# A decoder kernel: the feed-forward's first pair of token tiles is prepared in the last steps of the cross attention, and side jobs are pinned in DVE's queue

## The chip, the cores and the metric

The kernel runs on one core of a Trainium2 chip. The metric is the device time of one execution in microseconds (us), less is better. The engines are named as in the profile: PE (TensorE, matrix products and transposes), DVE (VectorE), ACT (ScalarE), POOL (GpSimd) and SP (SyncE, which here only issues DMAs). Each runs its own queue in order; semaphores make one wait for another.

## The reference

The reference is a decoder of two layers over 16 sequences of 128 tokens with 512 features. Each of its six parts is followed by a residual add and a layer norm: a state-space scan, a cross attention with 16 heads, a feed-forward with ternary weights and 8-bit activations, a causal attention with ternary weights ("BitLinear"), a gated cross attention and a mixture of experts. The change touches the seam between the second and the third part. The third is:

```python
def _L0_ffn_ref(x, W_g, W_u, W_d):
    def rms_norm(x, eps=1e-08):
        mean = jnp.mean(x, axis=-1, keepdims=True)
        var = jnp.var(x, axis=-1, keepdims=True)
        return (x - mean) / jnp.sqrt(var + eps)
    def activation_quant(x):
        s = 127.0 / jnp.max(jnp.abs(x), axis=-1, keepdims=True)
        return jnp.clip(jnp.round(s * x), -128, 127) / s
    def ternary_matmul(x, w):
        return jnp.matmul(x, jnp.sign(w).T)
    xq = activation_quant(rms_norm(x))
    g = jax.nn.silu(ternary_matmul(xq, W_g))
    u = ternary_matmul(xq, W_u)
    p = g * u
    return ternary_matmul(p, W_d)
...
x = _layernorm(x + _L0_xattn_ref(x, ctx_2048, ...), axis=-1)
x = _layernorm(x + _L0_ffn_ref(x, L0_ffn_W_g, L0_ffn_W_u, L0_ffn_W_d), axis=-1)
```

W_g and W_u are 2048 x 512, W_d is 512 x 2048.

## The kernel before

The tokens stay on the chip as 16 tiles `k.x[b]` of 128 tokens by 512 features. The stages run one after another over all 16 tiles; within the program the order on each engine is made by a scheduler from priorities (program order) and estimated costs, so an instruction whose inputs are ready can be put ahead of others that stand earlier in the program. An instruction handed to `keep_in_program_order` is not moved in this way.

**Cross attention** (`stage_xattn`, profile lines L450 to L614). One step handles a pair of heads of one tile; there are 128 such units, 8 per tile. A step computes scores (L555), maxima (L559), exponentials (L568, ACT), the normalization by the sums (L574, and L575 on POOL) and the transposes of the probabilities (L583), whose results ACT (L586) and DVE (L588) copy to `pTs`. The generator `outputs` makes the attention output `ao` (L595), its copy `aT` (L600) and the product with Wo, `po` (L606); after the last head group `po` is added to the token tile (L609) and, when both tiles of a pair are done, the pair is normalized (`layernorm`, L68 to L72). Side generators in the list `running` are advanced once per step: the projections of the next tile (`project`, with `rope` at L450 to L460) and the like. The last units belong to tiles 14 and 15. Its PSUM takes two banks each for projections (`pp`), scores (`psc`), transposes (`ppt`), and two for `ao` and `po`.

**Feed-forward** (`stage_ffn`). It works over pairs of tiles. `prepare` normalizes a pair (`xn`), finds each token's largest magnitude (L680), scales and rounds (`q_t`, L690, DVE, by adding a large constant; `q_q`, L691, ACT, by taking it away), transposes the result (L701, PE) and copies it (`q_T`, L703, ACT). The first pair is prepared before the loop; each later one in the loop, one piece at a time. In the loop, for each tile and each of four blocks of 512 hidden features, PE makes the gate and up products `pg` and `pu` (L755), ACT the Silu `sg` (L758), DVE the product `sg` (L759), PE its transposes (L375), ACT and DVE split them into `hi` (L764) and `lo` (L765), and PE adds their products with the down weights into `po` (L769), which is added to the token tile (L777). `load_ffn_weights` loads the weights through five rotating slots and ACT takes their signs (L659 for gate and up, L669 for down).

**Side jobs.** `ahead` holds work for the next stage: `load_bit_weights` (sums of magnitudes L807, then the ternary weights L820 to L822) and `load_gated_masks` (a maximum over the mask L834, the mask values L837 and L839). In the program the generator is advanced in the second half of a tile's blocks, from the second pair of tiles on; in the order that the scheduler makes, L807 and L834 to L839 stand at the start of the stage.

Of the kernel before, what the change touches and what calls it, by code (L numbers as in the profile page):

```python
# [10 lines left out]
F32 = mybir.dt.float32  # L11
BF16 = mybir.dt.bfloat16
# [3 lines left out]
AF = mybir.ActivationFunctionType  # L16
ALU = mybir.AluOpType
AX = mybir.AxisListType
PSUM = bass.MemoryType.PSUM

P = 128
NB = 16
D = 512
KC = D // P
NT = NB * P
MAGIC = 12582912.0
# [377 lines left out]
def stage_xattn(k):  # L404
# [9 lines left out]
    with ExitStack() as ctx:  # L414
# [175 lines left out]
        def outputs(st, g):  # L590
# [17 lines left out]
            if g == G - 1:  # L608
                nc.vector.tensor_tensor(k.x[st.b], st.po, k.x[st.b], ALU.add)  # L609
                yield  # L610
                if st.b % 2:
                    xs = k.x[st.b - 1 : st.b + 1]
                    layernorm(k, xs, xs)
                    yield  # L614

        def advance():
            for job in list(running):
                if next(job, running) is running:
                    running.remove(job)
# [3 lines left out]
        for t in range(-12, len(units) + 4):  # L623
            for lag, what in ((3, turn), (2, norm), (1, exps), (0, top), (-1, scores)):
                if not 0 <= t - lag < len(units):
                    continue
                b, g, i = units[t - lag]
                st = state[b]
                if what is scores and (g, i) == (0, 0):
                    st.b, st.sc, st.mx, st.pr, st.sm, st.pTs = b, {}, {}, {}, {}, {}  # L630
                what(st, g, i)
                if what is turn and i == 1:
                    running.append(outputs(st, g))
            b, r = divmod(t + 11, U)
            if r == 0 and b < NB:
                running.append(project(b))
            b, r = divmod(t + 15, U)
            if t == -12 or r == 0 and b > 0 and b < NB and b % 4 == 0:
                running.append(angles(max(b, 0) // 4))
            advance()  # L640
# [29 lines left out]
        k.fd.append(fd.rearrange("p (h e) -> p h e", h=8))  # L670


def quantize(k, ins, floor=None):


    nc, n = k.nc, len(ins)
    s = k.small.tile([P, n], F32, tag=f"qs{n}", name="qs")
    step = k.small.tile([P, n], F32, tag=f"qst{n}", name="qst")
    for i, x in enumerate(ins):
        nc.vector.tensor_reduce(s[:, i : i + 1], x, AX.X, ALU.max, apply_absolute_value=True)  # L680
    if floor is not None:
        nc.vector.tensor_scalar(s, s, floor, None, ALU.max)
    nc.vector.reciprocal(s, s)
    nc.vector.tensor_scalar(s, s, 127.0, None, ALU.mult)
    nc.vector.reciprocal(step, s)
    outs = []
    for i, x in enumerate(ins):
        t = k.wk.tile([P, D], F32, tag="q_t", name="q_t")
        q = k.wk.tile([P, D], BF16, tag="q_q", name="q_q")
        nc.vector.tensor_scalar(t, x, s[:, i : i + 1], MAGIC, ALU.mult, ALU.add)  # L690
        nc.scalar.activation(q, t, AF.Identity, bias=k.nmagic)  # L691
        outs.append(q)
    return outs, step


def transpose_q(k, pool, q):

    nc = k.nc
    pt = pool.tile([P, KC, P], BF16, tag="pp", name="ptq")
    for c in range(KC):  # L700
        nc.tensor.transpose(pt[:, c], q[:, c * P : (c + 1) * P], k.identb)  # L701
    qT = k.wk.tile([P, KC, P], BF16, tag="q_T", name="q_T")
    nc.scalar.copy(qT, pt)  # L703
    return qT


def stage_ffn(k):


    nc, tc = k.nc, k.tc  # L710
    HB = 4
    with ExitStack() as ctx:
        k.wk = wk = ctx.enter_context(tc.tile_pool(name="s3w", bufs=3))
        pg = ctx.enter_context(tc.tile_pool(name="s3g", bufs=2, space=PSUM))
        pp = ctx.enter_context(tc.tile_pool(name="s3p", bufs=2, space=PSUM))
        po_ = ctx.enter_context(tc.tile_pool(name="s3o", bufs=1, space=PSUM))
        raws = ctx.enter_context(tc.tile_pool(name="s3r", bufs=1))
        load_ffn_weights(k)
        ahead = chain(load_bit_weights(k, raws, po_), load_gated_masks(k, raws))

        def prepare(st):

            xn = [wk.tile([P, D], F32, tag="xn", name="xn") for _ in st.xs]
            layernorm(k, st.xs, xn, 1e-8)
            yield
            qs, st.step = quantize(k, xn)
            yield
            st.qT = []
            for q in qs:
                st.qT.append(transpose_q(k, po_, q))  # L730
                yield

        def finish(st):
            layernorm(k, st.xs, st.xs)
            yield

        states = []
        for b0 in range(0, NB, 2):
            st = Ctx()
            st.xs = k.x[b0 : b0 + 2]  # L740
            states.append(st)
        for _ in prepare(states[0]):
            pass
        late = iter(())
        for n, sn in enumerate(states):
            nxt = prepare(states[n + 1]) if n + 1 < len(states) else iter(())
            for i, x in enumerate(sn.xs):
                st = sn.step[:, i : i + 1]
                po = po_.tile([P, D], F32, tag="po", name="po")
                for h in range(HB):  # L750
                    ps = []
                    for w, tag in zip(k.fw, ("pg", "pu")):
                        p = pg.tile([P, D], F32, tag=tag, name=tag)
                        for c in range(KC):
                            nc.tensor.matmul(p, sn.qT[i][:, c], w[:, c, h * D : (h + 1) * D], start=c == 0, stop=c == KC - 1)  # L755
                        ps.append(p)
                    sg = wk.tile([P, D], F32, tag="sg", name="sg")
                    nc.scalar.activation(sg, ps[0], AF.Silu, scale=st)  # L758
                    nc.vector.scalar_tensor_tensor(sg, ps[1], st, sg, ALU.mult, ALU.mult)  # L759
                    pt = pp.tile([P, D], F32, tag="pt", name="pt")  # L760
                    transpose4(k, pt, sg)
                    hi = wk.tile([P, D], F32R, tag="hi", name="hi")
                    lo = wk.tile([P, D], F32R, tag="lo", name="lo")
                    nc.scalar.copy(hi, pt)  # L764
                    nc.vector.tensor_tensor(lo, pt, hi, ALU.subtract)  # L765
                    for part in (hi, lo):
                        for c in range(4):
                            hc = 4 * h + c
                            nc.tensor.matmul(  # L769
                                po, part[:, c * P : (c + 1) * P], k.fd[hc // 8][:, hc % 8],  # L770
                                start=part is hi and hc == 0, stop=part is lo and hc == 15,
                            )
                    next(late, None)
                    next(nxt, None)
                    if n and h >= 2:
                        next(ahead, None)
                nc.vector.tensor_tensor(x, po, x, ALU.add)  # L777
            late = finish(sn)
        for _ in late:
            pass  # L780


def load_bit_weights(k, raws, psum):
# [20 lines left out]
    views = [raw[:, :, 0:512], rawo, raw[:, :, 512:640], raw[:, :, 640:768]]  # L804
    tot = k.small.tile([P, 4], F32, tag="bw_tot", name="bw_tot", bufs=1)
    for i, w in enumerate(views):
        nc.vector.tensor_reduce(tot[:, i : i + 1], w, AX.XY, ALU.add, apply_absolute_value=True)  # L807
        yield
    pt = psum.tile([P, 4], F32, tag="pp", name="ptw")
    nc.tensor.matmul(pt, ones, tot, start=True, stop=True)  # L810
# [7 lines left out]
    outs = [wb[:, :, 0:512], wb[:, :, 768:1280], wb[:, :, 512:640], wb[:, :, 640:768]]  # L818
    for i, (w, o) in enumerate(zip(views, outs)):
        nc.vector.tensor_scalar(w, w, rsw[:, i : i + 1], MAGIC, ALU.mult, ALU.add)  # L820
        nc.vector.tensor_scalar(w, w, MAGIC, 1.0, ALU.subtract, ALU.min)
        nc.vector.tensor_scalar(o, w, -1.0, None, ALU.max)  # L822
        yield


def load_gated_masks(k, raws):


    nc, a, pool = k.nc, k.args, k.bit_pool
    m8 = raws.tile([P, NB, P], U8, name="m8")  # L830
    nc.sync.dma_start(m8, a["mask"].rearrange("b t -> (b t)").partition_broadcast(P).rearrange("p (b t) -> p b t", b=NB))
    yield
    k.gated_any = pool.tile([P, NB], F32, name="anyk")
    nc.vector.tensor_reduce(k.gated_any, m8, AX.X, ALU.max)  # L834
    yield
    k.gated_mask = mb = pool.tile([P, NB, P], BF16, name="mb")
    nc.vector.tensor_scalar(mb, m8, 1e30, -1e30, ALU.mult, ALU.add)  # L837
    yield
    nc.vector.tensor_tensor(mb, mb, k.gated_any.unsqueeze(2).to_broadcast([P, NB, P]), ALU.mult)  # L839
    yield  # L840


# [822 lines left out]
def decoder(ctx: ExitStack, tc: tile.TileContext, args):  # L1665
    k = Ctx()
    k.nc, k.tc, k.args = tc.nc, tc, args
    nc = tc.nc
# [29 lines left out]
    nc.scalar.preload_act_table_set("natural_log_exp_and_others")  # L1698
    actx = ctx.enter_context(ExitStack())
    for stage in STAGES:  # L1700
        if stage is stage_ffn:
            k.bit_pool = actx.enter_context(tc.tile_pool(name="bit", bufs=1))
        if stage is stage_attention:
            wctx.close()
            k.gated_pool = actx.enter_context(tc.tile_pool(name="gated", bufs=1))
        if stage is stage_moe:
            actx.close()
        stage(k)
# [77 lines left out]
```

## Time and profile before

| | us |
|---|---|
| median of 3 runs | 3400.72 |
| lowest and highest run | 3398.65, 3407.02 |
| the profiled execution | 3407.26 |
| its span, first to last instruction | 3405.5 |
| busy: PE | 3172.3 (93% of the span) |
| busy: DVE | 1894.7 (56%) |
| busy: ACT | 1373.7 (40%) |
| busy: POOL | 1391.6 (41%) |

The mean granted clock of PE is 0.964 of full speed. How to read the views: a group of instructions is given by its line, engine, operation and "output<-inputs"; in a timeline a row has its start, its length, and in brackets the idle time of its engine just before it and what ended it. A row that covers several instructions (x4) has them overlapping, so its length is a little more than the time from its start to the next row's. Times count from the start of the span. Cross attention ends on PE at about 1638 us, the feed-forward on PE runs from about 1657 to 1935 us.

### The profile page before, as it was taken

The page shows a single profiled execution, that of the slowest core. Times are in us where ns is not written, and L with a number is a line of the kernel's source. Part 1 is how long each engine was busy: PE and PEld are TensorE (multiplying, and loading weights), DVE is VectorE, ACT ScalarE, POOL GpSimd, SP SyncE. Part 2 cuts the span into 40 slices and gives each one's busy share as a digit, 9 for nine tenths or more (in the row PEclk, how much of TensorE's full clock was granted, in tenths as well). Part 3 has the DMA queues.
Part 4 walks back from the last instruction along what each step waited for, and adds up shares of the span by engine and source line. Part 5 has one row for each costly group of instructions (what it writes and reads, how often), then busy time and mean ns, then how long its engine had stood idle before and what let it go on. Part 6 is the DMA issues. An engine that isn't in the chain of part 4 may idle for free. (4 is left out here: it accounts for less than half of the span.)

```text
span 3405.5 us, 38787 instructions
## 1 busy us (share of the span) xinstructions
PE 3172.3 (93%) x12944; PEld 1817.4 (53%) x12944; DVE 1894.7 (56%) x4346; ACT 1373.7 (40%) x3283; POOL 1391.6 (41%) x1198
## 2 busy tenths in 40 slices
PE   6888999899999999999799899998889999999998
PEld 3444444455555555555466465665555566556665
DVE  5877888456456456455576589765543232222223
ACT  4645655133233333335333388865543231111221
POOL 6967887243333233332000165224624455233331
PEclk8999999999999999999899999998989999999999
DMA  7887332200000000003100100013435566445441
GB/s 237 259 254 217 96 87 68 67 7 4 7 4 7 4 4 7 4 1 124 59 1 1 62 1 1 10 59 119 152 131 179 195 223 201 166 152 174 159 159 65
DMA packets 161554, 317.29 MB, mean 93 GB/s; under 512 B 19113, under 2 KB 82089, under 8 KB 158276
## 3 DMA queue, kind: packets, MB, share of 16 engines
q1 hardware_dynamic: 123012, 215.83, 20.6%
q0 software_dynamic: 19328, 64.56, 5.6%
q10 hardware_dynamic: 19008, 34.35, 2.7%
q8 instruction: 105, 1.72, 0.2%
q14 instruction: 101, 0.83, 0.1%
HBM read 238.80 MB, written 129.04 MB: 108 GB/s over the span
## 5 line engine op out<-in xcount | busy, mean ns | idle before, releaser
L245 POOL TENSOR_TENSOR dBx<-dtx,BC 128x1024 f32<-128x1024 f32 x128 | 301.6, 2375 | 45.4 <-DVE h L258 36.8
L1522 PE MATMUL pg<-gu,xgT 128*128 128x352 f32 x784 | 301.7, 467 | 0.0
L1522 PE MATMUL pu<-gu,xgT 128*128 128x352 f32 x784 | 300.6, 466 | 0.0
L1539 PE MATMUL y<-dn,aT 128*128 128x512 f32 x588 | 268.3, 592 | 0.0
L1526 DVE SCALAR_TENSOR_TENSOR act<-pu,row,act 128x352 f32<-128x352 f32 x98 | 57.1, 583 | 377.7 <-PE pu L1522 327.0
L575 POOL TENSOR_TENSOR pr<-pr,sm 128x512 f32<-128x512 f32 x128 | 134.7, 1053 | 287.9 <-DVE sm L574 242.5
L236 ACT ACTIVATE h<-dt,negA 128x254 f32<-128x254 f32 x512 | 239.8, 474 | 14.9 <-DVE dt L178 2.1
L1565 POOL TENSOR_TENSOR x<-got,x 128x512 f32<-128x512 f32 x120 | 152.7, 1277 | 226.0 <-DMA got<-results,gidx 225.2
L606 PE MATMUL po<-w,aT 128*128 128x512 f32 x512 | 230.5, 593 | 1.1 <-DVE aT L600 1.1
L483 PE MATMUL pq<-w,xT 128*128 128x512 f32 x512 | 228.9, 594 | 0.0
L1558 POOL DMA_INDIRECT got<-results,gidx x120 | 116.1, 968 | 269.8 <-DMA results<-yo 248.2
L258 DVE TENSOR_TENSOR_SCAN h<-h,dBx 128x1024 f32<-128x1024 f32 x80 | 183.0, 2294 | 71.1 <-ACT h L236 48.8
L460 POOL TENSOR_TENSOR m<-m,m 128x512 f32<-128x512 f32 x96 | 121.6, 1267 | 244.2 <-DVE m L455 244.2
L568 ACT ACTIVATE pr<-sc,mx,sf 128x256 f32<-128x256 f32 x256 | 142.8, 562 | 187.0 <-DVE mx L561 176.1
L267 PE MATMUL py<-hC,ident 128*128 128x512 f32 x320 | 167.3, 652 | 54.6 <-ACT y L272 48.9
L1522 PEld LDWEIGHTS pu<-gu,xgT 128*128 128x128 f32 x784 | 151.5, 193 | 85.2 <-issue 4.4
L1522 PEld LDWEIGHTS pg<-gu,xgT 128*128 128x128 f32 x784 | 143.9, 194 | 65.1 <-issue 3.9
L1525 ACT ACTIVATE act<-pg 128x352 f32<-128x352 f32 x98 | 45.5, 464 | 318.8 <-PE pg L1522 256.8
L1539 PEld LDWEIGHTS y<-dn,aT 128*128 128x128 f32 x588 | 104.1, 190 | 100.8 <-issue 94.2
L1514 ACT COPY xgT<-ptx 128x512 f32<-128x512 f32 x98 | 57.5, 587 | 234.7 <-PE ptx L375 213.3
L483 PEld LDWEIGHTS pq<-w,xT 128*128 128x128 f32 x512 | 93.5, 190 | 102.0 <-issue 99.0
L606 PEld LDWEIGHTS po<-w,aT 128*128 128x128 f32 x512 | 94.8, 190 | 95.8 <-issue 91.8
(363 smaller groups left out, 6851.0 us busy)
## 6 DMA issues: line engine op xcount, KB each, us to landing
bucket<-zeros SPq DMA_DIRECT2D x96, 388.0 KB
row<-bucket SPq DMA_DIRECT2D x90, 388.0 KB
BC<-bcd SPq DMA_DIRECT2D x128, 256.0 KB
results<-yo ACTq DMA_DIRECT2D x90, 256.0 KB
gu<-in_moe_guT SPq DMA_DIRECT2D x16, 1408.0 KB
cT<-in_ctxT SPq DMA_DIRECT2D x32, 256.0 KB
dn<-in_moe_downT SPq DMA_DIRECT2D x16, 512.0 KB
rows<-r_row SPq DMA_DIRECT2D x16, 388.0 KB
```

The costliest lines, as they stand in the source:

```text
L236: nc.scalar.activation(h[:, c, :, 1:], st.dt[:, c].rearrange("p (b t) -> p b t", b=BQ)[:, :, 1:], AF.Exp, scale=negA[:, c, n : n + 1])
L245: nc.gpsimd.tensor_tensor(dBx, st.dtx, BC[:, 0].unsqueeze(1).to_broadcast([P, KC, TQ]), ALU.mult)
L258: nc.vector.tensor_tensor_scan(hf, hf, df, 0.0, ALU.mult, ALU.add)
L267: nc.tensor.matmul(st.py[c], k.ident, st.hC[n][:, 2 * c : 2 * c + 2], start=n == 0, stop=n == NS - 1)
L460: nc.gpsimd.tensor_tensor(m1, m1, m2, ALU.add)
L483: nc.tensor.matmul(ps, src[:, c], w[c], start=c == 0, stop=c == KC - 1)
L568: nc.scalar.activation(pr[:, j], st.sc[g, i][:, j], AF.Exp, scale=st.sf[:, h : h + 1], bias=st.mx[g, i][:, j : j + 1], accum_out=sm[:, j : ...
L575: nc.gpsimd.tensor_tensor(pr, pr, sm.unsqueeze(2).to_broadcast([P, 2, 2 * P]), ALU.mult)
L606: nc.tensor.matmul(st.po, aT[:, j], k.wo[h // 8][:, h % 8], start=h == 0, stop=h == G * J - 1)
L1522: nc.tensor.matmul(ps, u.xT[:, c], gu[:, c, lo : lo + I], start=c == 0, stop=c == KC - 1)
L1539: self.nc.tensor.matmul(u.y, u.aT[:, c], u.w[1][:, c], start=c == 0, stop=c == 2)
L1565: nc.gpsimd.tensor_tensor(k.x[b], got, k.x[b], ALU.add)
```

## The change

Two things are changed. First, the preparation of a pair is put into a function of its own, `prepare_ffn`, that takes a function `new` for its tiles. For the first pair (tiles 0 and 1, finished long before) it becomes a side generator of the cross attention, added four units ahead of the end of the units. Its tiles are those of the projections, which are over then (`m1`, `m2`, `sq`, and the PSUM tag `pt`), and a small pool `early` holds the two results `q_T`. The feed-forward's loop takes this state in place of the one that it prepared itself. Second, six DVE statements in the side jobs are handed to `keep_in_program_order`: the sums of magnitudes, two of the three steps that make the ternary weights, and the three mask steps.

```diff
@@ stage_xattn
+        def prepare_first():
+            homes = {"xn": (wk, "m1", 4), "q_t": (wk, "m2", 2), "q_q": (wk, "sq", 2), "pt": (ppt, "pt", 2), "q_T": (k.early, "q_T0", 2)}
+            st = k.ffn_first = Ctx()
+            st.xs = k.x[0:2]
+            def new(what, shape, dt):
+                pool, tag, bufs = homes[what]
+                return pool.tile(shape, dt, tag=tag, name=what, bufs=bufs)
+            return prepare_ffn(k, st, new)
...
+            if t == len(units) - 4:
+                running.append(prepare_first())
@@ the preparation, before in stage_ffn's prepare, quantize and transpose_q
+def prepare_ffn(k, st, new):
+    nc = k.nc
+    xn = [new("xn", [P, D], F32) for _ in st.xs]
+    layernorm(k, st.xs, xn, 1e-8)
+    yield
+    s = k.small.tile([P, 2], F32, tag="qs2", name="qs")
+    st.step = k.small.tile([P, 2], F32, tag="qst2", name="qst")
+    for i, x in enumerate(xn):
         nc.vector.tensor_reduce(s[:, i : i + 1], x, AX.X, ALU.max, apply_absolute_value=True)
     nc.vector.reciprocal(s, s)
     nc.vector.tensor_scalar(s, s, 127.0, None, ALU.mult)
+    nc.vector.reciprocal(st.step, s)
+    qs = []
+    for i, x in enumerate(xn):
+        t = new("q_t", [P, D], F32)
+        qs.append(new("q_q", [P, D], BF16))
         nc.vector.tensor_scalar(t, x, s[:, i : i + 1], MAGIC, ALU.mult, ALU.add)
+        nc.scalar.activation(qs[i], t, AF.Identity, bias=k.nmagic)
+    yield
+    st.qT = []
+    for q in qs:
+        pt = new("pt", [P, KC, P], BF16)
+        for c in range(KC):
+            nc.tensor.transpose(pt[:, c], q[:, c * P : (c + 1) * P], k.identb)
+        st.qT.append(new("q_T", [P, KC, P], BF16))
+        nc.scalar.copy(st.qT[-1], pt)
+        yield
@@ stage_ffn
-            st = Ctx()
+            st = Ctx() if b0 else k.ffn_first
             st.xs = k.x[b0 : b0 + 2]
             states.append(st)
-        for _ in prepare(states[0]):
-            pass
@@ load_bit_weights
-        nc.vector.tensor_reduce(tot[:, i : i + 1], w, AX.XY, ALU.add, apply_absolute_value=True)
+        k.tc.keep_in_program_order(nc.vector.tensor_reduce(tot[:, i : i + 1], w, AX.XY, ALU.add, apply_absolute_value=True))
...
         nc.vector.tensor_scalar(w, w, rsw[:, i : i + 1], MAGIC, ALU.mult, ALU.add)
-        nc.vector.tensor_scalar(w, w, MAGIC, 1.0, ALU.subtract, ALU.min)
-        nc.vector.tensor_scalar(o, w, -1.0, None, ALU.max)
+        k.tc.keep_in_program_order(nc.vector.tensor_scalar(w, w, MAGIC, 1.0, ALU.subtract, ALU.min))
+        k.tc.keep_in_program_order(nc.vector.tensor_scalar(o, w, -1.0, None, ALU.max))
@@ load_gated_masks
-    nc.vector.tensor_reduce(k.gated_any, m8, AX.X, ALU.max)
+    k.tc.keep_in_program_order(nc.vector.tensor_reduce(k.gated_any, m8, AX.X, ALU.max))
...
-    nc.vector.tensor_scalar(mb, m8, 1e30, -1e30, ALU.mult, ALU.add)
+    k.tc.keep_in_program_order(nc.vector.tensor_scalar(mb, m8, 1e30, -1e30, ALU.mult, ALU.add))
...
-    nc.vector.tensor_tensor(mb, mb, k.gated_any.unsqueeze(2).to_broadcast([P, NB, P]), ALU.mult)
+    k.tc.keep_in_program_order(nc.vector.tensor_tensor(mb, mb, k.gated_any.unsqueeze(2).to_broadcast([P, NB, P]), ALU.mult))
@@ decoder
+        if stage is stage_xattn:
+            k.early = actx.enter_context(tc.tile_pool(name="early", bufs=1))
```

The lines move by four to twelve: the Silu of L758 is L762 in the changed kernel, the sums L807 are L811, the mask steps L834, L837 and L839 are L838, L841 and L843, the down-weight signs L669 are L683. In the changed order of instructions, both parts of the preparation stand in DVE's queue between the steps of tile 15, the eight transposes in PE's queue between its last outputs, six gate and up products of the first tile stand ahead of the last two `po` groups, and L811 to L843 stand in the middle of the feed-forward. The queues of POOL and SP have the same instructions in the same order as before.

More of the change, by code (lines that the diff above doesn't have):

```diff
@@ L670, in load_ffn_weights @@
         k.fd.append(fd.rearrange("p (h e) -> p h e", h=8))
[L673 to L679, printed above, removed]
+def prepare_ffn(k, st, new):
[6 more added lines that the diff above has]
+    for i, x in enumerate(xn):
         nc.vector.tensor_reduce(s[:, i : i + 1], x, AX.X, ALU.max, apply_absolute_value=True)
-    if floor is not None:
-        nc.vector.tensor_scalar(s, s, floor, None, ALU.max)
     nc.vector.reciprocal(s, s)
     nc.vector.tensor_scalar(s, s, 127.0, None, ALU.mult)
[L685 to L704, printed above, removed]
+    nc.vector.reciprocal(st.step, s)
[3 more added lines that the diff above has]
+        qs.append(new("q_q", [P, D], BF16))
+        nc.vector.tensor_scalar(t, x, s[:, i : i + 1], MAGIC, ALU.mult, ALU.add)
+        nc.scalar.activation(qs[i], t, AF.Identity, bias=k.nmagic)
[8 more added lines that the diff above has]
+        yield
 def stage_ffn(k):
@@ L712, in stage_ffn @@
     with ExitStack() as ctx:
-        k.wk = wk = ctx.enter_context(tc.tile_pool(name="s3w", bufs=3))
+        wk = ctx.enter_context(tc.tile_pool(name="s3w", bufs=3))
         pg = ctx.enter_context(tc.tile_pool(name="s3g", bufs=2, space=PSUM))
@@ L721, in prepare, with new @@
         def prepare(st):
[L723 to L731, printed above, removed]
+            def new(what, shape, dt):
+                return po_.tile(shape, dt, tag="pp", name="ptq") if what == "pt" else wk.tile(shape, dt, tag=what, name=what)
+            return prepare_ffn(k, st, new)
         def finish(st):
```

## The prediction

> **What bounds the kernel now.** I read the page first: span, busy shares, 40 slices.
>
> ```profile
> span 3405.5 us, 38787 instructions
> ...
> PE   6888999899999999999799899998889999999998
> ```
>
> TensorE (PE) is the bound nearly everywhere; one slice between the cross attention and the feed-forward drops to 7. A time is won only where PE stands still, so the second view cuts that place into windows (columns: length, PE, weight loads, DVE, ACT, POOL busy, granted PE clock, DMA).
>
> ```profile
> 1620.00:1640.00 20.00, 17.24 (x48) 7.65 (x46) 4.83 (x8) 5.33 (x6) 1.26 (x4) 1.00 0.34 108
> 1640.00:1660.00 20.00, 2.17 (x11) 1.28 (x12) 20.00 (x65) 5.89 (x9) 0.00 (x0) 0.58 0.43 144
> 1660.00:1680.00 20.00, 19.91 (x92) 11.71 (x91) 8.88 (x13) 8.74 (x14) 0.00 (x0) 0.91 0.00 0
> ```
>
> In the middle window PE works 2.17 us and DVE all 20; the clock falls to half and is not whole in the next window. The waits of PE from 1620 to 1945 us (total, times, longest) name the place; from 1680 to 1920 PE waits for nothing.
>
> ```profile
> PE ptq L701 <- ACT q_q L691: 18.8, 1, 18.8
> ...
> PE po L606 <- DVE aT L600: 1.1, 2, 0.8
> ...
> PE ptq L701 <- ACT q_T L703: 0.7, 1, 0.7
> ```
>
> Then the timelines of the gap: PE, DVE, ACT.
>
> ```profile
> 1634.67 3.70 PE L606 MATMUL po<-w,aT 128*128 128x512 f32 x8 [0.78 <-DVE aT L600]
> 1657.16 0.61 PE L701 MATMUL ptq<-identb,q_q 128*128 128x128 bf16 x4 [18.79 <-ACT q_q L691]
> ...
> 1660.53 1.91 PE L755 MATMUL pu<-w,q_T 128*128 128x512 bf16 x4
> ...
> 1669.51 1.10 PE L769 MATMUL po<-w,lo 128*128 128x512 f32 x4
> ```
> ```profile
> 1645.34 2.28 DVE L807 TENSOR_REDUCE bw_tot<-l_raw 128x1 f32<-128x2048 f32 x1
> ...
> 1653.49 2.28 DVE L834 TENSOR_REDUCE anyk<-m 128x16 f32<-128x2048 uint8 x1
> ...
> 1655.76 0.86 DVE L690 TENSOR_SCALAR q_t<-xn,qs 128x512 f32<-128x512 f32 x2
> ```
> ```profile
> 1639.15 3.90 ACT L669 ACTIVATE w<-w 128x1024 fp32r<-128x1024 f32 x4 [9.25 <-DMA w<-in_ff_wdT]
> ...
> 1659.66 1.28 ACT L758 ACT_TABLE_LOAD   x1
> 1660.96 0.69 ACT L758 ACTIVATE sg<-pg,qst 128x512 f32<-128x512 f32 x1
> ```
>
> PE ends the cross attention at 1638.37 (1634.67 + 3.70) and starts the feed-forward at 1657.16. Between, DVE normalizes three pairs (cross-attention result, tokens 0/1, tokens 2/3) and does side jobs: 2.28 + 0.68 + 2.27 + 0.68 + 2.28 us (bit-weight sums, mask maximum) stand ahead of the q_t that PE waits for, 1.21 + 2.29 behind it: 11.69 us.
>
> **The change part by part.**
>
> *The preparation of tokens 0/1 moves ahead.* It removes from the gap two bn_stats (0.69), two aggregates, 11 small rsqrt steps, two xn (0.99 together), two maxima (1.27), two q_t (0.86), and on ACT two q_q (1.34) and two q_T copies (0.59 each). The order of the changed build puts the DVE part into the steps of before's 1582 to 1600 us, about 6 us of DVE. There DVE idles 0.6 to 2.2 us per step. Following the queue with before's durations, one bn_stats (0.6 us) goes ahead of the aT and pTs copies of 1583.3, and an aggregate and a step of rsqrt (0.3 together) go behind them; the pTs copy ends at about 1584.87 instead of 1584.60, and PE, which already waits 0.24 for it, loses 0.28. Later aT moves from 1592.05 to 1593.5 (PE needs it at 1594.05), and the two exps of the next step end about 1.5 us later, with more than 3 us until their transposes: nothing lost. POOL and SP get no new instruction and no new order; q_t waits only for POOL's L460, over since 1579.3.
>
> *Eight bf16 transposes* move into PE's last steps: 0.23 us per four (1671.32 to 1671.55), 0.46. *Six gate/up matmuls* go between the last po groups (0.216 each from 0.81 per overlapping three): they fill the two waits for aT (0.35, 0.78) and cost about 0.1. So the last L606 ends at 1638.37 + 0.28 + 0.46 + 0.1 = 1639.2.
>
> *What is late next.* ACT runs in order. Its second group of down-weight signs (L669, now L683) needs a DMA and the slot that the last L606 frees; the table load and the first Silu stand behind it. The first sign group waits for the first half of Wo, 0.73 later than before, so this DMA lands at 1639.15 + 0.73 = 1639.9. Signs 3.90: 1643.8; table load 1.28: 1645.1; Silu 0.69: 1645.75. DVE is free for sg by 1644.5 (before: 5.88 us from the L609 add to the L72 pair; less two bn_stats, two aggregates and some ten small steps, 2.1; plus 0.9 for the L72 pair and 0.5 for one xn). So ACT sets it. PE has ten gate/up matmuls left (2.16 us) until 1641.35; the next needs the bank that this Silu frees: **a new wait of 4.4 us**.
>
> *Restart, at full clock.* Two matmuls 1646.2; sg 1645.8 to 1646.5, xn, second sg to 1647.7; transposes to 1648.2. DVE now does the two maxima of the next pair (1.27) before lo: lo at 1649.55 and 1650.2, so the four groups of down products (0.95 each) end at 1652.45. Before had two more gate matmuls done by then: 0.43, 1652.9 against 1670.45 (end of the 1669.51 row). Gain 17.5.
>
> *The clock.* A 4.4 us gap may cool it. First a window of 1 us in before's gap (the clock is the third figure from the end), then PE's timeline in the state-space stage:
>
> ```profile
> 1643.00:1644.00 1.00, 0.00 (x0) 0.00 (x0) 1.00 (x17) 0.04 (x1) 0.00 (x0) 0.59 1.10 341
> ```
> ```profile
> 88.35 3.78 PE L267 MATMUL py<-hC,ident 128*128 128x512 f32 x4 [4.39 <-DVE hC L259]
> ```
>
> With full clock in the window before and 0.50 after, 0.59 puts the fall at about 1643.2, 4.8 us after PE's end at 1638.37; by that row alone 4.4 us stays warm, gain 17.5. But after the 4.39 us gap in the state-space stage four matmuls took 3.78 us where such a one takes 0.65 on average. [...] I take cold. [...] Gain 15.5 (14.7 to 16.2).
>
> *Pinned side jobs.* The seven jobs (11.69 us) now stand in the feed-forward, from the second pair on. The rows nearest are the other side jobs (L820 to L822, 1.2 us each) at 1750 to 1765: DVE was busy 16.18 and 18.59 of 20 us there and PE 19.99 and 20.00, cost nothing. Their data is there: the trace shows no wait of DVE for a load even in the gap. For a 2.28 us job I followed one place in the new order: after the third lo of tile 3, DVE does the job and sg (2.95 us together) while PE has 2.67 us of products plus 0.4 of slack. Bounds: nothing (even a gain is excluded, PE is full) and 11.69. Taken 1, by the L820 rows.
>
> Sum: 15.5 - 1.0 = **14.5 us**. The profiled execution took 3407.26 (span 3405.5 and 1.8 around it), 6.5 above the median 3400.72 and just above the highest run, 3407.02; its rows hold nothing in this gap that would scale with that. So 3392.8 against it, 3386.2 against the median.
>
> **The rivals.**
> 1. *Warm restart*, chance 0.12. For: the fall at 4.8 us. Against: the 4.39 row. Gain 17.5 - 1 = 16.5: 3384.2.
> 2. *Half of it eaten*, 0.22: DVE's 6 extra us make PE late in more steps than one, or some side jobs reach PE. For: PE's transposes follow sg by 0.06 us in places (sg ends 1672.34, transposes 1672.40). Against: scheduled fillers. Gain 5 to 11, 8: 3392.7.
> 3. *Slower*, 0.07: the side jobs stop PE in the feed-forward. Place: the sg behind each of five jobs of 1.2 to 2.3 us. [...] Against: the filled windows above.
> 4. *The preparation isn't early*: its waits (POOL's L460, ACT's exps ahead of its q_q) hold it back, and only the side jobs ahead of q_t leave the gap, 8.2 us: 3392.5. Against: POOL is done with L460 at 1579.3. It lies inside rival 2.
>
> **How the numbers follow.** Likeliest (0.59): cold restart, 3386.2, its own range 3383 to 3390. The 80% range takes rival 1 and about 3 us of run scatter (3398.65 to 3407.02 shown) below, most of rival 2 above: 3380 to 3395. A measurement of this kernel can tell about 0.3%, 10.2 us. Faster by more: likeliest and rival 1 nearly whole, a third of rival 2, less scatter: 0.78. Within: 0.15. Slower: 0.07.
>
> **What would show it.** Right: one PE wait of 4 to 5.5 us for ACT (the Silu, L762) near 1641, none of 18.8; table load straight behind four signs; half clock for 3 to 8 us; reduces L811 and L838 at 1700 to 1850 with PE still 20.00 of 20. Wrong: PE waits for aT, pTs or pr between 1582 and 1620 above 1 us; PE waits for sg or lo in the feed-forward above 2 us in sum; an end of the gap set by DVE.

## The result and the profile after

The changed kernel took 3386.6 us (median of 6 runs, 3382.8 to 3392.7), the kernel before beside it 3402.27: a ratio of 0.9953, 95% interval 0.9943 to 0.9963. The forecast was 3386.2. By the medians the gain is 15.7 us, where 14.5 was forecast.

The page and the cut into windows of the changed kernel (columns as before). The 20th slice, which holds the seam, is 9 where it was 7; the 7 of now is the 23rd, at the next stage's beginning:

```profile
span 3384.7 us, 38731 instructions
...
PE   6888999899999999999999798998889999999998
```
```profile
1620.00:1640.00 20.00, 16.45 (x48) 7.09 (x48) 7.56 (x33) 9.08 (x9) 1.26 (x4) 1.00 0.52 173
1640.00:1660.00 20.00, 19.04 (x81) 11.94 (x83) 9.75 (x21) 8.00 (x13) 0.00 (x0) 0.83 0.24 79
1660.00:1680.00 20.00, 19.95 (x97) 12.37 (x97) 10.71 (x23) 6.28 (x10) 0.00 (x0) 1.00 0.00 1
```

In the middle window PE works 19.04 us instead of 2.17. Of PE's waits from 1620 to 1945 us, these belong to the seam and the feed-forward (total, times, longest):

```profile
PE pg L759 <- ACT sg L762: 4.2, 1, 4.2
...
PE po L773 <- ACT hi L768: 1.0, 2, 0.7
...
PE pt L375 <- DVE sg L763: 0.2, 1, 0.2
```

The 18.8 us wait is gone; one of 4.2 us stands in its place. The timelines of PE, ACT and DVE there:

```profile
1617.30 1.04 PE L583 MATMUL pT<-ident,pr 128*128 128x128 f32 x8
...
1630.64 3.70 PE L606 MATMUL po<-w,aT 128*128 128x512 f32 x8
...
1635.48 1.03 PE L759 MATMUL pu<-w,q_T 128*128 128x512 bf16 x4
1640.74 1.01 PE L759 MATMUL pg<-w,q_T 128*128 128x512 bf16 x2 [4.24 <-ACT sg L762]
1641.68 2.23 PE L375 MATMUL pt<-ident,sg 128*128 128x128 f32 x8
```
```profile
1634.79 3.90 ACT L683 ACTIVATE w<-w 128x1024 fp32r<-128x1024 f32 x4 [8.91 <-PE pu L759]
1638.71 1.28 ACT L762 ACT_TABLE_LOAD   x1
1640.00 1.27 ACT L762 ACTIVATE sg<-pg,qst 128x512 f32<-128x512 f32 x2
```
```profile
1634.38 0.69 DVE L609 TENSOR_TENSOR x<-po,x 128x512 f32<-128x512 f32 x1 [3.79 <-PE po L606]
...
1639.16 1.00 DVE L72 TENSOR_SCALAR x<-x,ln_mv,rs_y 128x512 f32<-128x512 f32 x2
...
1640.88 0.75 DVE L763 SCALAR_TENSOR_TENSOR sg<-pu,qst,sg 128x512 f32<-128x512 f32 x1
```

ACT makes four signs, loads its table and comes to the first Silu, while PE stands; DVE comes free for the first product at almost the same time. Two readings were thus possible of who sets the wait. The eight transposes of the restart (L375) then take 2.23 us, twice the 1.04 us that eight f32 transposes take in a row in the cross attention (L583): the clock has fallen, to 0.50 of full speed by the windows from 1640 to 1646 us. For the end of ACT's wait ahead of the signs the profile names `pu`, which the signs do not read. In eight of the eleven traces in which the four signs stand in this place it names the weights' DMA instead.

To separate the change from what other stages did, I measure one stretch in each trace: from the first row of the last tile's query projection to the first attention mask. (The expectations quoted below call its start the last state-space row of pq; it is line L483 of the cross attention.) These are the two rows of the changed kernel:

```profile
1554.54 7.11 PE L483 MATMUL pq<-w,xT 128*128 128x512 f32 x16
...
1914.67 1.04 PE L995 MATMUL sc<-mask,identb 128*128 128x512 bf16 x4
```

360.13 us, where the kernel before has 375.06 (1560.29 to 1935.35): **14.93 us gained in the stretch**. The remaining 5.75 us by which the changed kernel's first row is earlier arose ahead of the change's place.

### The profile page after: what moved, and what is told of

Read it like the earlier page. It is cut to its first block, busy times and chain, and to the rows that moved or that the text cites. A ratio compares the mean times of both kernels' runs of the same rounds, so it can differ in the third digit from the quotient of the medians.

```text
span 3384.7 us, 38731 instructions
## 1 busy us (share of the span) xinstructions
PE 3166.2 (94%) x12893; PEld 1819.4 (54%) x12944; DVE 1887.2 (56%) x4346; ACT 1373.3 (41%) x3283; POOL 1391.4 (41%) x1198
## 3 DMA queue, kind: packets, MB, share of 16 engines
q8 instruction: 105, 1.72, 0.2%
## 5 line engine op out<-in xcount | busy, mean ns | idle before, releaser
L575 POOL TENSOR_TENSOR pr<-pr,sm 128x512 f32<-128x512 f32 x128 | 134.7, 1053 | 289.3 <-DVE sm L574 236.7
L606 PE MATMUL po<-w,aT 128*128 128x512 f32 x512 | 230.7, 593 | 0.5 <-DVE aT L600 0.5
L483 PE MATMUL pq<-w,xT 128*128 128x512 f32 x512 | 228.9, 594 | 0.0
L483 PEld LDWEIGHTS pq<-w,xT 128*128 128x128 f32 x512 | 93.5, 190 | 102.0 <-issue 99.0
L606 PEld LDWEIGHTS po<-w,aT 128*128 128x128 f32 x512 | 94.7, 190 | 95.3 <-issue 91.8
```

Source lines behind the costliest of these rows:

```text
L483: nc.tensor.matmul(ps, src[:, c], w[c], start=c == 0, stop=c == KC - 1)
L575: nc.gpsimd.tensor_tensor(pr, pr, sm.unsqueeze(2).to_broadcast([P, 2, 2 * P]), ALU.mult)
L606: nc.tensor.matmul(st.po, aT[:, j], k.wo[h // 8][:, h % 8], start=h == 0, stop=h == G * J - 1)
```

## The experiments

All times in this table are counted from the first row of the stretch. "Cold" is the time at half clock, summed over windows as their length times (1 - granted clock) / 0.5. The ratio is of the medians to the kernel before.

| kernel | last L606 starts | PE restarts after its wait | cold | stretch | ratio, 95% interval |
|---|---|---|---|---|---|
| before (again) | 74.38 (74.38) | 96.87 (96.87) | 20.48 (20.48) | 375.06 (374.87) | 1 |
| changed (again) | 76.10 (75.96) | 86.20 (86.30) | 6.82 (6.82) | 360.13 (360.05) | 0.9953 (0.9943 to 0.9963) |
| pins alone | 74.37 | 89.77 | 13.65 | 367.50 | 0.9979 (0.997 to 0.9988) |
| preparation alone | 75.97 | 86.84 | 6.82 | 360.13 | 0.9947 (0.9934 to 0.996) |
| idle gap filled | 75.98 | 86.01 | 0 | 357.49 | 0.9958 (0.9945 to 0.997) |
| signs late | 75.95 | no wait | 0 | 352.28 | 0.9933 (0.992 to 0.9946) |
| norm late (again) | 75.73 (75.75) | 85.62 (86.05) | 3.42 (3.41) | 358.44 (359.03) | 0.9956 (0.994 to 0.9971) |
| both late | 75.73 | no wait | 0 | 351.97 | 0.9932 (0.9919 to 0.9945) |
| two norms on ACT (again) | 75.18 (75.18) | 85.35 (85.60) | 3.42 (6.84) | 357.52 (359.00) | 0.9957 (0.9944 to 0.997) |
| signs late, two norms on ACT | 75.18 | no wait | 0 | 351.22 | 0.9933 (0.992 to 0.9946) |

The times of whole runs scatter by about 0.3%, so differences of 2 to 3 us between two changed kernels are read from the stretch alone.

**1. How far one trace's stretch is to be trusted.** Both kernels run again without an edit.

> The changed kernel once more, unaltered, to see how far one trace's stretch (last state-space row of pq to first attention mask, 360.13 us) can be trusted. Two runs with a like wait of TensorE were cold for 3.4 us, where the changed kernel's first trace shows 6.7 us. Theory (the clock is granted by windows of about 3.4 us, whose place against the program differs from run to run): the same instruction order, wait 4.0 to 4.3 us, and a stretch of 358.3 to 360.5 us, by whether one or two windows are cold. Rival (the cold time follows from the program alone): 360.1 within 0.2 us, 6.7 us cold.

> The kernel before once more, unaltered: the stretch was 375.06 us. Theory (as for the changed kernel, one window of the clock more or less): 373.5 to 376 us, with the wait of 18.8 us unchanged within 0.3. Rival (it repeats exactly): 375.06 within 0.2.

The rival came out: 360.05 and 374.87, within 0.2 us, and the same cold times. The wait was 4.49 us this time, a little over what was expected.

**2. The pins alone**: the kernel before with the six `keep_in_program_order`, the preparation left in the gap.

```diff
-        nc.vector.tensor_reduce(tot[:, i : i + 1], w, AX.XY, ALU.add, apply_absolute_value=True)
+        k.tc.keep_in_program_order(nc.vector.tensor_reduce(tot[:, i : i + 1], w, AX.XY, ALU.add, apply_absolute_value=True))
...
```

> The kernel before with the six pins alone: the first pair's preparation stays between the last po and the first gate matmul. Theory (the wait was DVE's own chain, with 8.2 us of side jobs in it ahead of the last q_t): about 7 to 8 us faster than before, the stretch from the last state-space row of pq to the first attention mask falling from 375.06 to about 367 to 368 us, and the wait of the first gate transposes from 18.8 to some 11 us. Rival (pins do nothing since the jobs are due within the feed-forward anyway and DVE pays for them later): under 1 us faster. If all of the changed kernel's 14.9 us came from the pins, this would give it; no theory expects that.

375.06 - 367.50 = 7.56 us gained. PE's waits of this kernel, first row:

```profile
PE ptq L701 <- ACT q_q L691: 11.7, 1, 11.7
```

The five jobs that stood ahead of q_t (8.2 us by their rows) leave, the wait falls by 7.1 us, and PE is cold for 6.83 us less (13.65 against 20.48). So in the kernel before the side jobs were about two fifths of the wait.

**3. The preparation alone**: the changed kernel without the pins.

```diff
-        k.tc.keep_in_program_order(nc.vector.tensor_reduce(tot[:, i : i + 1], w, AX.XY, ALU.add, apply_absolute_value=True))
+        nc.vector.tensor_reduce(tot[:, i : i + 1], w, AX.XY, ALU.add, apply_absolute_value=True)
...
```

> The changed kernel without the six pins: the preparation is early, but the side jobs are free to slide into DVE's queue around the new gap (the built order has one 2.3 us sum ahead of the first product, another ahead of the second transposed remainder, and 7.5 us more before the first po is added). Theory (DVE and ACT both end the new gap at about the same time): 2 to 6 us slower than the changed kernel, so 9 to 13 us faster than before, with the wait at the first product 4.2 us grown to about 6 and new PE waits on DVE's L769. Rival (ACT alone ends the gap, DVE has room): the same as the changed kernel within 1 us.

The stretch is 360.13 us, as in the changed kernel; the rival was right. DVE's timeline shows a side job ahead of the first product, and PE's shows longer waits, 5.00 us for the Silu instead of 4.24 and 0.92 us for DVE's `sg` instead of 0.19:

```profile
1642.33 2.29 DVE L811 TENSOR_REDUCE bw_tot<-l_raw 128x1 f32<-128x2048 f32 x1
1644.54 0.74 DVE L763 SCALAR_TENSOR_TENSOR sg<-pu,qst,sg 128x512 f32<-128x512 f32 x1
```
```profile
1643.59 2.72 PE L759 MATMUL pg<-w,q_T 128*128 128x512 bf16 x6 [5.00 <-ACT sg L762]
1646.10 1.06 PE L375 MATMUL pt<-ident,sg 128*128 128x128 f32 x4
...
1913.57 0.66 PE L375 MATMUL pt<-ident,sg 128*128 128x128 f32 x4 [0.92 <-DVE sg L763]
```

Neither of the two comes from that side job. The wait for the Silu is longer mainly because the DMA let the signs start 0.64 us later (80.89 against 80.25 us into the stretch), and the wait for DVE stands in the last block of the feed-forward. The job does make the first product 1.45 us later (87.79 against 86.34), but PE fills the time: it makes six gate products ahead of the transposes, where the changed kernel makes two. PE makes the two longer waits up again within the feed-forward; in which steps was not followed, and why the stretches agree to the hundredth is open. The two parts of the change do not add: 7.56 alone and 14.93 alone give 14.93 together, for both shorten the same wait, and once the preparation is out of it, the pinned jobs no longer stand in a place that matters.

**4. What the fallen clock costs**: 18 more gate-shaped matmuls, whose result nothing reads, in the gap.

```diff
+                    if (n, i, h) == (0, 0, 2):
+                        idle = po_.tile([P, D], F32, tag="pp", name="idle")
+                        for _ in range(18):
+                            nc.tensor.matmul(idle, sn.qT[0][:, 0], k.fw[0][:, 0, 0:D], start=True, stop=True)
```

> The changed kernel with 18 more matmuls of the gate's shape, whose result nothing reads, in the 4.2 us in which TensorE waits for the first product. Theory (the clock falls since TensorE stands still, and the restart then runs at half clock for 6.5 us): granted clock 1.00 through 1640 to 1647, and 1.5 to 2.5 us faster than the changed kernel (stretch 360.1 to about 358). Rival (the restart is paced by ACT and DVE, not by TensorE's clock): the same within 0.5 us, with the clock at 1.00 and longer waits of TensorE in its place.

PE's timeline and windows of this kernel (clock third from the end):

```profile
1642.38 4.05 PE L758 MATMUL idle<-w,q_T 128*128 128x512 bf16 x18
1646.72 0.81 PE L763 MATMUL pg<-w,q_T 128*128 128x512 bf16 x3 [0.29 <-ACT sg L766]
1647.72 0.66 PE L375 MATMUL pt<-ident,sg 128*128 128x128 f32 x4 [0.20 <-DVE sg L767]
```
```profile
1644.00:1646.00 2.00, 2.00 (x11) 0.88 (x9) 2.00 (x15) 1.97 (x3) 0.00 (x0) 1.00 1.07 373
1646.00:1648.00 2.00, 1.51 (x8) 0.57 (x6) 1.81 (x5) 1.25 (x2) 0.00 (x0) 1.00 1.12 345
```

Four transposes take 0.66 us again, the clock stays whole, and the stretch is 2.64 us shorter, although PE did 4 us more of useless work. That is the price of the 6.82 us at half clock, a little above the 1.5 to 2.5 us expected. ACT's chain was hardly shortened: PE restarts at 86.01 us, against 86.20 and 86.30 in the two traces of the changed kernel.

**5. ACT alone: the second half of the down weights' signs late**, behind the first blocks' gates.

```diff
-        for c in range(4):
-            nc.scalar.activation(fd[:, c * 1024 : (c + 1) * 1024], raw[:, c * 1024 : (c + 1) * 1024], AF.Sign)
+        def signs(fd=fd, raw=raw):
+            for c in range(4):
+                nc.scalar.activation(fd[:, c * 1024 : (c + 1) * 1024], raw[:, c * 1024 : (c + 1) * 1024], AF.Sign)
+        if i == 0:
+            signs()
+        k.second_signs = signs
...
+                    if (n, i, h) == (0, 0, 2):
+                        k.second_signs()
```

> The changed kernel with the second half of the down weights' signs (4 of ACT's instructions, 3.9 us) put behind the first four blocks' gates, so that ACT's table load and first gates stand ahead of them. Theory (DVE's layer norm of the last pair ends at 1640.9 as well, so that taking ACT away uncovers DVE): the wait at the first product shrinks by at most 0.5 us, and the total is within 1 us of the changed kernel. Rival (ACT alone sets it, as the prediction said): the table load moves up by the 3.9 us, the wait falls to under 1 us, the clock stays up, and the kernel is 4 to 6 us faster than the changed one.

My theory fell, and its rival came out larger than it said: the stretch is 7.85 us shorter than the changed kernel's. ACT's and DVE's timelines:

```profile
1642.23 1.28 ACT L768 ACT_TABLE_LOAD   x1 [8.62 <-PE po L606]
1643.52 1.27 ACT L768 ACTIVATE sg<-pg,qst 128x512 f32<-128x512 f32 x2
1644.68 2.00 ACT L684 ACTIVATE w<-w 128x1024 fp32r<-128x1024 f32 x2
```
```profile
1644.71 0.15 DVE L53 TENSOR_SCALAR rs_a<-ln_mv 128x2 f32<-128x2 f32 x1
1644.77 0.74 DVE L769 SCALAR_TENSOR_TENSOR sg<-pu,qst,sg 128x512 f32<-128x512 f32 x1
1645.43 0.16 DVE L54 TENSOR_SCALAR rs_y<-rs_a 128x2 int32<-128x2 int32 x1
```

The table load is at 1642.23 - 1562.43 = 79.80 us of the stretch instead of 84.17. And DVE's product no longer stands behind the layer norm: the scheduler now puts it into the middle of it, since its input is ready. So DVE's layer norm stood in front in the changed kernel because ACT was late. PE has no wait left between 1610 and 1700 us, and its cold time is 0. Of the 7.85 us the wait is 4.24, the clock 2.64 by experiment 4; where the last 1 us comes from was not measured.

**6. DVE alone, and both**: the last layer norm moved from `outputs` to the second tile's start in the feed-forward, without and with the late signs.

```diff
-                if st.b % 2:
+                if st.b % 2 and st.b < NB - 1:
...
+                    if (n, i, h) == (0, 1, 0):
+                        layernorm(k, k.x[NB - 2 : NB], k.x[NB - 2 : NB], keep=True)
```

> The changed kernel with the cross attention's last layer norm (the last pair of tiles, on VectorE, 1635 to 1640 in the changed kernel's trace) moved behind the second tile's start in the feed-forward, ScalarE's queue left as it is. Theory (four signs and the table load on ScalarE end the new wait alone; VectorE stood in front only because ScalarE's gate was late anyway): the wait at the first product stays within 0.3 us of 4.2, the stretch from the last state-space row of pq to the first attention mask within 1 us of 360.1. Rival (VectorE's norm is a second, equal cause): the wait shrinks by more than 0.5 us and the stretch by more than 1.5 us.

> The second half of the down weights' signs late and the last layer norm late as well. Theory (the signs alone were the cause): within 1 us of the run with the signs late alone, a stretch of 352.3 us, the moved norm being hidden beside TensorE in either place. Rival (VectorE's first product still waited for tiny norm instructions, 0.9 us in the run with the signs late): 1 to 2 us shorter than 352.3. On the other side, the norm pinned inside the feed-forward could hold back a product there: up to 2 us longer.

With the norm late and the signs left, ACT's and DVE's timelines read:

```profile
1643.19 3.90 ACT L685 ACTIVATE w<-w 128x1024 fp32r<-128x1024 f32 x4 [8.71 <-DMA w<-in_ff_wdT]
1647.11 1.28 ACT L764 ACT_TABLE_LOAD   x1
1648.40 1.27 ACT L764 ACTIVATE sg<-pg,qst 128x512 f32<-128x512 f32 x2
```
```profile
1649.13 1.41 DVE L765 SCALAR_TENSOR_TENSOR sg<-pu,qst,sg 128x512 f32<-128x512 f32 x2 [1.65 <-ACT sg L764]
```

DVE is idle for 1.65 us and waits for ACT: PE's wait is still 4.03 us. So ACT sets it, and what ACT waits for at the start is the weights' DMA, as the prediction put it. But the stretch is 1.69 us shorter, more than the theory allowed (1.10 in the second trace, experiment 8). Of the 1.69, 0.37 lies ahead of the gap (75.73 against 76.10), and PE is cold for 3.42 us instead of 6.82. With both late the stretch is 351.97, 0.31 under the signs alone: DVE's part is nothing once ACT's is gone.

**7. The stall in the cross attention.** The last L606 started 1.72 us later in the changed kernel than before (76.10 against 74.38), where 0.83 was forecast. DVE's and POOL's timelines of the changed kernel show the part that was not foreseen:

```profile
1581.91 1.08 DVE L57 SCALAR_TENSOR_TENSOR rs_t<-rs_t,rs_a 128x2 f32<-128x2 f32 x2
...
1585.04 0.94 DVE L58 SCALAR_TENSOR_TENSOR rs_y<-rs_t,rs_y 128x2 f32<-128x2 f32 x1
...
1588.13 0.68 DVE L600 COPY aT<-ao 128x512 f32<-128x512 f32 x1
```
```profile
1581.90 1.07 POOL L575 TENSOR_TENSOR pr<-pr,sm 128x512 f32<-128x512 f32 x1 [5.28 <-DVE rs_t L56]
1584.93 1.04 POOL L575 TENSOR_TENSOR pr<-pr,sm 128x512 f32<-128x512 f32 x1 [1.96 <-DVE rs_t L56]
```

The row of 1.08 us covers two steps of rsqrt (one of them the preparation's), the longer of which took 0.96; the row of 0.94 is one step. Both long steps work on two numbers per partition and end with POOL's normalization beside them; the others around them take 0.15 or 0.16 us. In the kernel before no L57 or L58 between 1580 and 1605 us takes above 0.18. But earlier in its cross attention the same is to be seen. Of its 306 rsqrt steps (L56 to L58) between 690 and 1560 us, 14 took 0.90 to 1.05 us, where the medians are 0.17; each stood beside an L575 on POOL and ended with it, as these two rows do:

```profile
1535.25 1.04 DVE L58 SCALAR_TENSOR_TENSOR rs_y<-rs_t,rs_y 128x8 f32<-128x8 f32 x1
```
```profile
1535.23 1.04 POOL L575 TENSOR_TENSOR pr<-pr,sm 128x512 f32<-128x512 f32 x1 [1.86 <-DVE rs_t L57]
```

So the trace of the kernel before could have given the price. In the changed kernel the copy `aT` comes late and PE waits 0.50 us for it. For a test, two of these normalizations are made on ACT:

```diff
+            if (st.b, g, i) in units[-8:-6]:
+                for j in range(2):
+                    nc.scalar.activation(pr[:, j], pr[:, j], AF.Identity, scale=sm[:, j : j + 1])
+                return
             nc.gpsimd.tensor_tensor(pr, pr, sm.unsqueeze(2).to_broadcast([P, 2, 2 * P]), ALU.mult)
```

> The changed kernel with two of GpSimd's normalisations of probabilities (L575), those that stand beside the preparation's rsqrt, made on ScalarE in two instructions each. Theory (VectorE's L57 and L58, which read two operands from SBUF, stood still for as long as GpSimd ran: 1.08 us beside 1.07, 0.94 beside 1.04): both take the usual 0.16 to 0.3 us, aT (L600) of the unit comes 1.6 us earlier, the 0.50 us wait of L606 on it goes, and the last L606 starts 0.5 to 0.7 us earlier (76.1 us after the last pq row now). Rival (the two rows only look long, since they wait for operands): the rows and the wait stay, the last L606 within 0.2 us of 76.1. By the total alone the two can hardly be told apart.

> The second half of the signs late and the two normalisations on ScalarE, a candidate for a faster version. Theory: the two gains add, since one lies ahead of the first feed-forward matmul and one behind it: a stretch of about 351.7 us (352.3 with the signs late alone), 23 us faster than before. Rival (the time saved in the cross attention only lengthens the wait for the down weights' transfer): within 0.2 us of 352.3.

Only the second of the two collisions was taken away; the first belongs to a unit earlier, which stayed on POOL, and serves as the control. DVE and POOL:

```profile
1591.35 1.08 DVE L57 SCALAR_TENSOR_TENSOR rs_t<-rs_t,rs_a 128x2 f32<-128x2 f32 x2
...
1594.49 0.16 DVE L58 SCALAR_TENSOR_TENSOR rs_y<-rs_t,rs_y 128x2 f32<-128x2 f32 x1
```
```profile
1591.34 1.07 POOL L579 TENSOR_TENSOR pr<-pr,sm 128x512 f32<-128x512 f32 x1 [5.28 <-DVE rs_t L56]
```

Where POOL still runs, the pair takes 1.08 us; where it does not, the step takes 0.16. The 0.50 us wait of PE is gone, and the last L606 starts at 75.18 us in both traces of this kernel, 0.92 and 0.78 us earlier than in the two traces of the changed kernel. The two stalls together made `aT` late, and taking one out was enough to end the wait; the other was not tried alone. What is left, 0.80 us later than before, is what the prediction forecast (0.83). The two long steps read two inputs each, while a reciprocal of L574, with one input, ran in 0.17 us beside POOL (1592.82 in the changed kernel, beside a POOL row of 1592.04 to 1594.17); whether the number of inputs decides, no run tested.

With the late signs added the stretch is 351.22 us, 1.06 under the signs alone, of which 0.77 lies ahead of the gap: the two gains add. It is the shortest stretch of all, 23.8 us under the kernel before. The three kernels with late signs have ratios of 0.9932 and 0.9933; the changed kernel had 0.9953 and, again, 0.9951. By the run times alone the intervals still touch (0.992 to 0.9946 and 0.9943 to 0.9963).

**8. Is the length of the cold time set by the program?** Two of the kernels once more.

> The changed kernel with the last layer norm late, once more. Its first trace was cold for 3.42 us against 6.82 in both traces of the changed kernel, and 1.69 us shorter. Theory (the program sets where the clock's window falls against the restart): cold 3.42 us again, a stretch of 358.44 within 0.2. Rival (the window's place is chance): 6.82 us cold and 359.4 to 360, since one window at half clock is worth up to 1.7 us of TensorE's work.

> The changed kernel with two normalisations on ScalarE, once more. Theory (the program sets it): last L606 at 75.2 us after the last pq row, cold 3.42 us, a stretch of 357.52 within 0.2. Rival (chance): last L606 at 75.2 again, since that is VectorE's order, but 6.82 us cold and a stretch of 358.5 to 359.2.

Chance has a part in it. The two normalizations on ACT were cold for 3.42 us in the first trace and 6.84 in the second, with the second stretch 1.48 us longer, of which 0.25 is the later restart. The windows of the first and of the second trace:

```profile
1649.00:1650.00 1.00, 0.67 (x2) 0.10 (x1) 1.00 (x2) 0.86 (x2) 0.00 (x0) 0.75 1.10 350
1650.00:1652.00 2.00, 2.00 (x8) 1.39 (x8) 2.00 (x5) 0.59 (x1) 0.00 (x0) 0.50 1.06 379
1652.00:1653.00 1.00, 1.00 (x5) 0.88 (x4) 1.00 (x2) 0.53 (x1) 0.00 (x0) 0.55 0.93 293
```
```profile
1645.00:1646.00 1.00, 0.34 (x1) 0.10 (x1) 0.90 (x2) 1.00 (x2) 0.00 (x0) 0.53 1.07 361
1646.00:1651.00 5.00, 5.00 (x16) 3.61 (x15) 4.89 (x12) 1.44 (x4) 0.00 (x0) 0.50 0.60 208
1651.00:1652.00 1.00, 1.00 (x4) 0.77 (x3) 0.28 (x1) 1.00 (x2) 0.00 (x0) 0.55 0.00 0
```

The norm late was cold for 3.42 and 3.41 us, as the first theory said; its stretch was 0.59 us longer the second time, with a wait of 4.44 instead of 4.03, which neither expectation gave.

## Why the prediction was right, point by point

- **The gap and its new wait.** One wait for the Silu, 4.4 us forecast, 4.24 and 4.49 measured. The step "ACT sets it" holds by experiments 5 and 6: without the four signs the wait goes, without DVE's norm it stays at 4.03.
- **When DVE is free.** Forecast 1644.5, which is 84.2 us into the stretch; the first product started at 86.34. Of these 2.1 us, 0.9 is the later end of the cross attention. Another 1.0 is the layer norm: from the add L609 to the L72 pair it took 4.78 us (1634.38 to 1639.16), where 3.78 was counted (5.88 less 2.1). The removed instructions had stood between the rsqrt steps; with them gone these steps, each of which needs the one before it in its chain, start 0.08 to 0.12 us apart (1638.49, 1638.57, 1638.69, 1638.77), and the norm became 1.1 us shorter instead of 2.1. The term cost next to nothing, since the Silu, for which PE waited, ended at 86.15.
- **The clock.** Cold was taken on one row of the state-space stage. The fall 4.8 us after PE's end spoke against it. The clock fell in all seven traces with this wait (4.03 to 5.00 us). The 4.8 was no threshold: in the ten traces in which the clock fell, it did so 3.3 to 4.9 us after PE's last work, 3.3 in the changed kernel's first. No run shows what a cold restart is counted with in the gain of 15.5; it was the author's estimate. The runs showed 6.82 us at half clock in both traces of the changed kernel, in the first until 1646.65, 92.1 us into the stretch. Warm instead of cold was put at 2.0 us and measured 2.64. The forecast sign, half clock for 3 to 8 us, holds the 6.82 us of here and the 3.41 and 3.42 us of three traces of two other kernels with waits of 4.03 to 4.44 us; the shorter cold time is worth about 1.5 us by the two traces of experiment 8.
- **The end of the restart.** Gain to the end of the four groups of down products: 15.5 forecast; 1649.02 plus two gate matmuls (0.43) is 94.91 us into the stretch, before 110.16 (1670.45), so 15.25.
- **The cross attention's end.** The term mis-sized most: 0.83 forecast, 1.72 measured. The step that failed is that aT "moves from 1592.05 to 1593.5 (PE needs it at 1594.05)": it counted DVE's instructions and not that one of them, beside POOL, took 0.94 us, where it took 0.16 without. The prediction says that POOL's queue does not change, which is true, and stops there. Experiment 7 shows it. The loss went on through the chain behind it: the first group of signs started 1.73 us later than before (67.44 against 65.71), where 0.73 was forecast, and the DMA of the second group was issued 1.75 us later (1625.9 and 1629.9). Its signs then started 1.39 us later, at 80.25 us where 79.61 was forecast, since from the issue to the signs it took 8.9 us instead of 9.3; that this was shorter is luck. PE restarted at 86.20 us, where 85.46 was forecast, and the restart took 0.4 us less than forecast.
- **The side jobs.** 1 us forecast; the rest of the feed-forward lost 15.25 - 14.93 = 0.3, and without the pins the stretch is the same. The pins' share, put at 8.2 us in the fourth rival, is 7.56 alone and nothing beside the early preparation.
- **The rivals.** There was no warm restart, and nothing like half of the gain was eaten. PE was busy 19.54 to 19.95 of every 20 us from 1680 to 1900, so the slower case did not come near. The preparation was early.

The sum, 14.5, met 14.93 with its errors partly cancelling, and that is luck: about 1 us too little was counted as lost ahead of the first signs, a faster DMA and a faster restart took most of that up again (0.4 us each), and 0.7 too much was counted for the side jobs. The mechanism (the 18.8 us wait gone, a wait of 4.2 us for ACT and a cold restart in its place) was the forecast one.

## What to carry to other kernels

When two things are taken out of one wait, try each alone: their gains need not add, and the second may be worth nothing. After such a change read the queue of the engine that ends the new wait from its end backward, here Silu, table load, signs, DMA: moving four signs behind the first gates shortened the stretch by another 7.85 us, half of what the whole change had given. An instruction moved beside another engine's work is not priced by its own length only (here 0.94 us beside POOL, 0.16 without): look which engines run in the place where it goes, and whether the same instruction is much longer than its median somewhere in the trace already.

## What the runs showed of the hardware that was not expected

- **Cold time came in whole units of 3.41 us.** 3.42, 6.82, 13.65 and 20.48 us are 1, 2, 4 and 6 of them; what sets the unit is not shown. In the seven traces with a wait of 4.0 to 5.0 us the clock always fell. Where it fell after PE had restarted (0.15 to 0.43 us after; the moment of the fall is taken from windows of 0.1 us), there was one cold unit; where it fell before (0.59 to 1.37 us before), there were two. In the second trace of the two normalizations on ACT PE was busy for 2.8 of the first 3.4 us at half clock, and the clock stayed there for another 3.4; in the second trace of norm late PE had been busy for 0.43 us after its wait when the clock fell. In two traces of one kernel, one cold unit and two made stretches of 357.52 and 359.00 us.
- **A DVE step of 0.16 us took about 1 us** beside a POOL instruction (0.94 and 0.96 in the changed kernel, up to 1.05 in the kernel before), and the profile shows it as busy, not as waiting. Here only the comparison with its like and with POOL's rows showed it.
